# Weight sums on VectorE, mT evicted by two engines, a last turn of its own, and batch statistics in two parts: one change to a four-layer graph kernel

## The chip, the cores and the metric

The kernel runs on one core of a Trainium2 chip. The metric is device time in microseconds (us) of one execution. The kernel before the change takes 2664.24 us, the median of three runs from 2663.99 to 2666.74; the profiled execution spans 2665.5 us, and every time of a view below counts from its start.

## What is computed

x is 128 graphs of 128 nodes with 256 features, adj one 128 by 128 matrix, all in float32. Four layers follow each other, each as x = x + layer(relu(layernorm(x))). Cut to what matters:

```python
# layer 0: gated messages                       (h = relu(layernorm(x)))
m_in  = (a_in  @ h + eb ) * sigmoid(h @ gate_w)
m_out = (a_out @ h + oeb) * sigmoid(h @ out_gate_w)
x = x + relu(m_in + m_out + h * sigmoid(h @ loop_gate))
# layer 1: causal attention of one head, adj added to the scores
x = x + softmax(mask(q k^T / 16 + adj)) v Wo
# layer 2: three graph convolutions, 256 -> 512 -> 1024 -> 256
u = relu(A @ (h @ W1)); u = relu(A @ (u @ W2)); x = x + A @ (u @ W3)   # A = adj * adj
# layer 3: aggregate, linear, batchnorm, relu, linear, batchnorm
z = (A_hat @ h) @ bW1.T + b1;  z = relu(batchnorm(z))    # over all 128*128 rows
o = z @ bW2.T + b2;            x = x + batchnorm(o)
```

The two batch norms of layer 3 need mean and variance over all 16384 rows before their scale can be applied. So they cut the kernel into passes.

## The kernel before

**Tiling.** Four graphs make a group of T = 512 rows, and there are NG = 32 groups. Pass one takes every group through layers 0 to 2 and through the first linear of layer 3 (z); z goes to HBM except for the last group, 31, which stays in SBUF. Pass two takes z group by group (31 first, then 0 to 30: `ORDER`), applies the batch norm and relu on ScalarE, and multiplies by bW2; o stays in SBUF. Pass three applies the second batch norm, turns o by TensorE transposes, adds x3 and writes out.

**Seven products.** Every large product runs as seven half-size products on quarters (Winograd's form of Strassen's method) instead of eight. `seven` (L385) writes that list: seven matmul groups, with ScalarE copying three partial results (`kept`, L392) and VectorE or ScalarE putting four quarters together. The data side needs four elementwise sums (`sums`, L337, on VectorE). The weight side needs four more (`seven_of`, L198), made once per weight, on GpSimd: w1 (L263), w2 and w3 (L265, L266), the two attention weights (L259), bW1 (L294) and bW2 (L271).

**Streams and the written order.** Each layer is a generator that yields after each small step. One letter of a string takes one step of one generator: A and B are layers 0 and 1 (with the first part of layer 2) of later groups, C the rest of layer 2 of group g, D layer 3 of group g-1; b and d are the first step (the norm) of a further group of layers 1 and 3. `TURN` (L674) is the order for each of the 32 turns, `FILL` (L683) the order of the head, which brings the first groups to where turn 0 starts; there p is `prepare` (L237), which makes the weights ready. In turn 31 there is no A or B left, so that the same string leaves C, D and one d, and what remains of layer 3 of group 31 runs alone behind it (L701).

**The planner.** The order written is a priority, not a final order. At build time a planner puts each engine's instructions in a fixed sequence by estimated durations: what it believes ready may go ahead of earlier work that is not. In the trace the sum of L276, of the sixth step of `prepare`, runs at 9.95 us, ahead of work written long before it. On the chip each engine then works off its sequence in order.

**Names of the change.** `norm` (L305) takes mean and variance on VectorE (L311, L313), the inverse root on GpSimd (L315 to L319) and writes h by four ScalarE instructions (L322). `mixed` (L327) multiplies the node dimension by an adjacency matrix into a PSUM bank for each chunk of 128 features and evicts it; its callers give the engine: ScalarE for mT of layer 2's input (L561), VectorE for uT (L580) and gT (L648). `pu_x` to `pu_z` are the products of mT with W1. The first, pu_x, reads chunk 0 of mT, the second, pu_y, chunk 1, and the others their sums ms. `bn_affine` (L705) makes scale and shift from `bn_stats` rows, one of six numbers for each group, by one `bn_aggr` for each channel chunk (L710) over all 32 groups: four for the first batch norm (192 numbers each), two for the second.

The instructions of the mixed product with its eviction, and of a norm's end, are the ones that a reader should keep in view:

```python
pm[:, b, :], src[:, b, c * P : (c + 1) * P], aT        # L333, TensorE
evict(dst[:, c, :], pm.rearrange("p b n -> p (b n)"))    # L335
nc.scalar.activation(h[:, b, :], xt[:, b, :], AF.Relu, bias=..., scale=...)   # L322
```

Of the kernel before, what the change touches and what calls it, by code (L numbers as in the profile page):

```python
# [8 lines left out]
FP = mybir.dt.float32  # L9
AF = mybir.ActivationFunctionType  # L10
ALU = mybir.AluOpType
# [4 lines left out]
P = 128  # L16
LN_EPS = 1e-5
BN_EPS = 1e-5
# [4 lines left out]
def kernel(  # L23
# [39 lines left out]
    nc = tc.nc  # L63
    B, N, D = x.shape
    G = 4
    NG = B // G
    T = G * N
    DC = D // P
# [5 lines left out]
    FC = F1 // P  # L74
    assert N == P and T == 512 and D == 256 and H1 == 512 and B % G == 0

    const = ctx.enter_context(tc.tile_pool(name="const", bufs=1))
# [41 lines left out]
    a2T = const.tile([P, P], FP, name="a2T")  # L119
    ahT = const.tile([P, P], FP, name="ahT")  # L120
# [5 lines left out]
    stats1 = const.tile([P, FC, NG, 6], FP, name="stats1")  # L126
    stats2 = const.tile([P, DC, NG, 6], FP, name="stats2")
# [32 lines left out]
    an, anT, dscr, f = (part_of(wide1, P) for _ in range(4))  # L160
# [17 lines left out]
    for v in (b1, g1, be1, b2, g2, be2):  # L178
        k = v.shape[0] // P
# [3 lines left out]
    def inv_sqrt(dst, src, eps):  # L183

        if eps:
            nc.vector.tensor_scalar(dst, src, eps, None, ALU.add)
            src = dst
        nc.gpsimd.tensor_tensor(dst, src, nhalf[:, : dst.shape[1]], ALU.pow)
# [9 lines left out]
    def seven_of(b, name, extra=None):  # L198


        b11, b21, b12, b22 = quarters(b)
        if extra is None:
            extra = weights.tile([P, 3, b.shape[1] // 2, b.shape[2] // 2], FP, name=f"{name}_s")
        operands = set_of(b, extra)
        t4n, t1, t2 = operands[3:6]
        nc.gpsimd.tensor_tensor(t1, b12, b11, ALU.subtract)
        nc.gpsimd.tensor_tensor(t2, b22, t1, ALU.subtract)
        nc.gpsimd.tensor_tensor(t4n, b21, t2, ALU.subtract)
        nc.gpsimd.tensor_tensor(b12, b22, b12, ALU.subtract)
        return operands  # L210

    BW2T = scratch.tile([P, FC, D], FP, name="BW2T")
# [111 lines left out]
            )  # L324
        return h

    def mixed(dst, src, aT, name, evict):  # L327

        for c in range(src.shape[-1] // P):
            pm = bank([P, G, P], f"{name}_{c}")  # L330
            for b in range(G):
                nc.tensor.matmul(  # L332
                    pm[:, b, :], src[:, b, c * P : (c + 1) * P], aT, start=True, stop=True  # L333
                )
            evict(dst[:, c, :], pm.rearrange("p b n -> p (b n)"))  # L335

    def sums(engine, a, extra, s3=None):  # L337

# [137 lines left out]
    def layer1(g):  # L476
# [81 lines left out]
        h = norm(g, 2)  # L558
        yield
        mT = w.tile([P, DC, T], FP, tag="dT", name=f"mT_{g}", bufs=2)  # L560
        mixed(mT, h, a2T, f"pm2_{g}", nc.scalar.copy)  # L561
        ex = w.tile([P, 3, 1, T // 2], FP, tag="ex", name=f"ms_{g}", bufs=2)
        ms = sums(nc.vector, quarters_t(mT), ex)
        yield
# [12 lines left out]
            rows_by_half(ms, SETS["1"], H1 // 2), put, [P, 2, H1 // 2], f"pu_{g}"  # L577
        )
        uT = w.tile([P, HC1, T], FP, tag="uT", name=f"uT_{g}", bufs=1)
        mixed(uT, u, a2T, f"pmu_{g}", nc.vector.tensor_copy)  # L580
        ex = w.tile([P, 3, HC1 // 2, T // 2], FP, tag="us", name=f"us_{g}", bufs=1)
        US[g] = sums(nc.vector, quarters_t(uT), ex)
        yield
# [59 lines left out]
    def layer3(g):  # L643

        h = norm(g, 3)
        yield
        gT = w.tile([P, DC, T], FP, tag="dT", name=f"gT_{g}", bufs=2)
        mixed(gT, h, ahT, f"pg_{g}", nc.vector.tensor_copy)  # L648
        ex = w.tile([P, 3, 1, T // 2], FP, tag="ex", name=f"gs_{g}", bufs=2)
        gs = sums(nc.vector, quarters_t(gT), ex)  # L650
        yield
        z = ZT[g] = [zp.tile([P, 2, T], FP, tag="z", name=f"zo_{g}_{j}") for j in range(2)]
        done = []

        def put(ij, pb, other):
            i, j = ij
            dst = z[j][:, :, i * T // 2 : (i + 1) * T // 2]
            if other is None:
                nc.scalar.copy(dst, pb)
            else:  # L660
                nc.vector.tensor_tensor(dst, pb, other, ALU.add)
            done.append(j)
            if done.count(j) == 2:
                for jj in range(2):
                    nc.vector.bn_stats(stats1[:, 2 * j + jj, g, :], z[j][:, jj, :])
                if g != LAST:
                    nc.sync.dma_start(Z[g][:, 2 * j : 2 * j + 2, :], z[j])

        yield from seven(columns_by_half(gs, SETS["b"], 0), put, [P, 2, T // 2], f"pz_{g}")

    TURN = "CCCBCCABBDABBCABBDDCBADCDDBDCCDBACBCCABCCACbBCBBCBCBBCBCBCdB"  # L674
    US = {}
    AHEAD = 3

# [2 lines left out]

    FILL = "apaapaaaaBBABBBBBBBpBABBBApBABBpABBpABBABB"  # L683
    stream = {"a": layer0(0), "p": prepare(), "B": layer1(0), "A": part(layer0, 1)}
    for k in FILL:
        next(stream[k])
# [3 lines left out]
    for g in range(NG):  # L690
        if g + AHEAD < NG:
            load_x(g + AHEAD)
        stream = {
            "A": part(layer0, g + 2), "B": bs, "C": layer2(g), "D": ds,
            "b": part(layer1, g + 2), "d": layer3(g),
        }
        for k in TURN:
            next(stream[k], None)
        assert all(next(stream[k], k) == k for k in "ABCD")
        bs, ds = stream["b"], stream["d"]  # L700
    for _ in ds:  # L701
        pass
    passA.close()

    def bn_affine(stats, nch, gam, bet, name, bias=None):  # L705


        mv = const.tile([P, nch, 2], FP, name=f"mv_{name}")
        for j in range(nch):
            nc.vector.bn_aggr(mv[:, j, :], stats[:, j].rearrange("p g s -> p (g s)"))  # L710
        mean = mv[:, :, 0]
        if bias is not None:
            mean = const.tile([P, nch], FP, name=f"mean_{name}")
            nc.vector.tensor_tensor(mean, mv[:, :, 0], bias, ALU.add)
        sc = const.tile([P, nch], FP, name=f"sc_{name}")
        inv_sqrt(sc, mv[:, :, 1], BN_EPS)
        nc.vector.tensor_tensor(sc, sc, gam, ALU.mult)
        sh = const.tile([P, nch], FP, name=f"sh_{name}")
        nc.vector.tensor_tensor(sh, mean, sc, ALU.mult)
        nc.vector.tensor_tensor(sh, bet, sh, ALU.subtract)  # L720
        if bias is not None:
            part = const.tile([P, nch], FP, name=f"part_{name}")
            nc.vector.tensor_tensor(part, bias, sc, ALU.mult)
            nc.vector.tensor_tensor(sh, sh, part, ALU.add)
        return sc, sh


# [27 lines left out]
    def second(g):  # L755

        zl, zr = ZT[g]
        ex = zw.tile([P, 2, FC // 2, T // 2], FP, tag="zs", name=f"zs_{g}")
        a11, a21, a12, a22 = (z[:, :, i * T // 2 : (i + 1) * T // 2] for z in (zl, zr) for i in range(2))
        s1, s2 = ex[:, 0], ex[:, 1]  # L760
        a_r = a11, a12, a12, a22, s1, s2, a21
        for j in range(FC):
            z = ZT[g][j // 2][:, j % 2, :]
            nc.scalar.activation(  # L764
                z, z, AF.Relu, bias=sh1[:, j : j + 1], scale=sc1[:, j : j + 1],
            )
            yield
        nc.vector.tensor_tensor(s1, a21, a22, ALU.add)
        nc.vector.tensor_tensor(a21, a11, a21, ALU.subtract)
        nc.vector.tensor_tensor(s2, s1, a11, ALU.subtract)  # L770
        yield

        def product(r, pb, first):
            for c in range(FC // 2):
                nc.tensor.matmul(  # L775
                    pb, BW2R[r][:, c, :], a_r[r][:, c, :],
                    start=(first and c == 0), stop=(c == FC // 2 - 1), skip_group_check=True,
                )
            if r == 1:
                nc.vector.tensor_tensor(a12, a12, s2, ALU.subtract)  # L780

        done = []

        def put(ij, pb, other):
            i, j = ij
            dst = O[g][:, j, i * T // 2 : (i + 1) * T // 2]
            if other is None:
                nc.scalar.copy(dst, pb)
            else:
                nc.vector.tensor_tensor(dst, pb, other, ALU.add)  # L790
            done.append(j)
            if done.count(j) == 2:
                nc.vector.bn_stats(stats2[:, j, g, :], O[g][:, j, :])

        yield from seven(product, put, [P, T // 2], f"po_{g}", zw)

    for n in range(1, 1 + AT_ONCE):
        load_z(n)
    sc1, sh1 = bn_affine(stats1, FC, g1_c, be1_c, "bn1", b1_c)
    PREPARE = FC + 1  # L800
    now = second(LAST)
    for _ in range(PREPARE + 1):
        next(now)
    for n, g in enumerate(ORDER):
        then = second(ORDER[n + 1]) if n + 1 < NG else iter(())
        for _ in range(PREPARE):
            next(now)
            next(then, None)
        next(then, None)
        for _ in now:  # L810
            pass
        now = then
        if n + 1 + AT_ONCE < NG:
            load_z(n + 1 + AT_ONCE)
        if n % 4 == 3 and n // 4 < EARLY:
            load_x3(n // 4, x3p, "x3")
# [7 lines left out]

    for g in range(EARLY, EARLY + LATE):
        load_later(g)
    sc2, sh2 = bn_affine(stats2, DC, g2_c, be2_c, "bn2", b2_c)
    for g in range(NG):
        x3 = R[g]
        for i in range(DC):  # L830
# [52 lines left out]
```

## Time and profile before

| Part of the span | us | what runs |
|---|---|---|
| head, to the first product of turn 0 (first p_x of L377 at 98.57) | 98.6 | FILL |
| 32 turns | about 2252 | TURN; 71.65 us from turn to turn in the middle |
| end of pass one, from the last C step to the first po_x (2351 to 2380.5) | 29.5 | layer 3 of group 31, first batch norm |
| pass two (2380.5 to 2584.7) | 204 | 32 groups, some 6.2 us each |
| second batch norm and pass three (2584.7 to 2665.5) | 81 | transposes and writes; DMA at 322 GB/s or more from 2580 on |

The profile's first part gives TensorE (PE) 2541.2 us of 2665.5 (95%), VectorE (DVE) 1904.5 (71%), ScalarE (ACT) 1298.8 (49%), GpSimd (POOL) 317.0 (12%). A stretch in which PE is near its full length is read as bound by TensorE: there, other engines' work matters only if PE waits for it. In the view by stretches, PE is busy 71.04 of the 71.65 us of a middle turn, while it stands idle for some 50 of the first 140. The chain of waits names TensorE for 81% of the span. A line of the timeline reads: start, length, engine, line, operation, output<-inputs, shape, count, and in brackets the idle time before it with what ended it.

### The profile page before, as it was taken

Reading aid. Unit: us, or ns where it says so; the run is one execution under the profiler, and the core shown is the slowest. Engines: PE = TensorE matmul, PEld = TensorE weight load, DVE = VectorE, ACT = ScalarE, POOL = GpSimd, SP = SyncE. Lnnn points to the kernel's source line nnn. Section 1 sums busy time; section 2 is a strip of 40 time slices with the busy share of each in tenths; the row PEclk is TensorE's granted clock in tenths of the full one; section 3 lists DMA queues with packets and bytes.
Section 4 is the critical chain, followed back from the end, with each engine's and each line's share of the span. In section 5 each row is a group of like instructions: output and inputs, shape, how many; then the busy total and the mean of one; then the engine's idle time right before and its main releaser. Section 6 shows DMA issues by size and latency. Waiting matters only on the chain.

```text
span 2665.5 us, 40593 instructions
## 1 busy us (share of the span) xinstructions
PE 2541.2 (95%) x15215; PEld 2283.0 (86%) x15215; DVE 1904.5 (71%) x4743; ACT 1298.8 (49%) x2607; POOL 317.0 (12%) x616
## 2 busy tenths in 40 slices
PE   3899999999999999999999999999999999979984
PEld 2799999989998898999999899988989999968873
DVE  7677777777777777777777777777777776557775
ACT  3454444444455444454444444544454543336655
POOL 4111111111011110111111111111101111000011
PEclk7899999999999999999999999999999999989998
DMA  3000000000000000000000000000000000034469
GB/s 129 15 33 24 25 33 33 33 32 25 25 33 32 32 33 33 33 25 24 32 33 32 32 25 27 29 33 32 32 33 33 28 13 25 32 112 170 171 209 362
DMA packets 62055, 143.05 MB, mean 54 GB/s; under 512 B 4626, under 2 KB 39972, under 8 KB 57892
## 3 DMA queue, kind: packets, MB, share of 16 engines
q1 hardware_dynamic: 51636, 105.60, 11.1%
q0 software_dynamic: 9216, 33.56, 3.2%
q8 instruction: 120, 1.97, 0.3%
q10 hardware_dynamic: 1008, 1.31, 0.2%
q14 instruction: 75, 0.61, 0.1%
HBM read 73.48 MB, written 66.98 MB: 53 GB/s over the span
## 4 chain that ended last, share of the span: by engine, by line
PE 81%; DVE 6%; ACT 4%; DMA 4%; POOL 3%; issue 1%; ACTq 0%; POOLq 0%; DVEq 0%; SPq 0%
PE p_x L377 15%; PE p_z L377 8%; PE p_x L360 7%; PE pu_x L360 4%; PE pmu L332 4%; PE pz_x L377 4%; PE p_y L377 4%; PE po_x L775 3%; PE p_z L360 2%; ACT h L322 2%; PE pg L332 2%; PE pm L469 2%; PE py L551 2%; PE pqv_x L501 2%; PE pqv_x L496 2%; PE ps L521 2%
## 5 line engine op out<-in xcount | busy, mean ns | idle before, releaser
L322 ACT ACTIVATE h<-x,sh,rs 128x256 f32<-128x256 f32 x512 | 268.6, 589 | 386.4 <-POOL sh L319 386.4
L377 PE MATMUL p_x<-uT,w 128*128 128x256 f32 x1024 | 242.1, 379 | 0.0
L608 ACT ACTIVATE h2T<-h2T 128x512 f32<-128x512 f32 x192 | 120.4, 627 | 230.2 <-DVE h2T L607 230.2
L377 PEld LDWEIGHTS p_x<-uT,w 128*128 128x128 f32 x1024 | 189.6, 190 | 23.1
L315 POOL TENSOR_SCALAR rs<-mv 128x4 f32<-128x4 f32 x128 | 29.7, 232 | 1386.9 <-ACT h2T L608 1025.7
L311 DVE BATCH_NORM_STATS2 st<-x 128x6 f32<-128x256 f32 x512 | 190.4, 414 | 4.3 <-DMA x<-in_x_dram 2.1
L429 DVE SCALAR_TENSOR_TENSOR gs<-h,gw 128x256 f32<-128x256 f32 x384 | 163.3, 425 | 34.8 <-ACT h L322 28.8
L392 ACT COPY p_t<-p_x 128x512 f32<-128x512 f32 (+1 forms) x192 | 96.7, 504 | 114.6 <-PE p_x L377 101.9
L316 POOL TENSOR_TENSOR rs<-rs,nhalf 128x4 f32<-128x4 f32 x128 | 147.7, 1154 | 0.0
L332 PEld LDWEIGHTS pmu<-a2T,u 128*128 128x128 f32 x1024 | 119.5, 192 | 17.1 <-PE pr L636 7.4
L360 PEld LDWEIGHTS p_x<-w,h2T 128*128 128x128 f32 x1024 | 124.3, 192 | 3.3
L360 PE MATMUL p_x<-w,h2T 128*128 128x128 f32 x1024 | 124.6, 275 | 0.0
L574 ACT ACTIVATE u<-u 128x512 f32<-128x512 f32 x96 | 60.4, 631 | 131.8 <-DVE u L573 131.8
L764 ACT ACTIVATE zi<-zi,sh_bn,sc_bn 128x512 f32<-128x512 f32 x124 | 97.4, 812 | 55.4 <-DMA zi<-z 35.5
L332 PE MATMUL pmu<-a2T,u 128*128 128x128 f32 x1024 | 119.8, 275 | 1.8 <-ACT u L574 1.8
L377 PE MATMUL p_x<-us,w_s 128*128 128x256 f32 x512 | 121.3, 379 | 0.0
L377 PE MATMUL p_z<-us,w 128*128 128x256 f32 x512 | 121.2, 379 | 0.0
L377 PE MATMUL p_x<-uT,w_s 128*128 128x256 f32 x512 | 121.0, 379 | 0.0
L377 PE MATMUL p_y<-uT,w 128*128 128x256 f32 x512 | 121.0, 379 | 0.0
L377 PE MATMUL p_z<-us,w_s 128*128 128x256 f32 x512 | 121.0, 379 | 0.0
L377 PEld LDWEIGHTS p_z<-us,w 128*128 128x128 f32 x512 | 97.2, 190 | 13.5 <-ACT p_t L392 0.3
L377 PEld LDWEIGHTS p_z<-us,w_s 128*128 128x128 f32 x512 | 97.3, 190 | 13.2
(282 smaller groups left out, 6140.8 us busy)
## 6 DMA issues: line engine op xcount, KB each, us to landing
z<-zo SPq DMA_DIRECT2D x62, 512.0 KB, 2.6
zi<-z SPq DMA_DIRECT2D x31, 1024.0 KB, 4.8
x<-in_x_dram SPq DMA_DIRECT2D x32, 512.0 KB, 3.9
x<-x POOLq DMA_DIRECT2D x32, 512.0 KB, 3.0
x3i<-x POOLq DMA_DIRECT2D x32, 512.0 KB, 6.6
out_dram<-x3i SPq DMA_DIRECT2D x64, 256.0 KB, 8.3
w<-in_L_gnn_W_dram SPq DMA_DIRECT2D x1, 2048.0 KB
w<-in_L_gnn_W_dram SPq DMA_DIRECT2D x1, 1024.0 KB
```

Source lines behind the costliest of these rows:

```text
L311: nc.vector.bn_stats(st[:, b, :], xt[:, b, :])
L316: nc.gpsimd.tensor_tensor(rs, rs, nhalf[:, :G], ALU.pow)
L322: nc.scalar.activation(h[:, b, :], xt[:, b, :], AF.Relu, bias=sh[:, b : b + 1], scale=rs[:, b : b + 1])
L332: nc.tensor.matmul(pm[:, b, :], src[:, b, c * P : (c + 1) * P], aT, start=True, stop=True)
L360: nc.tensor.matmul(pb[:, rr, :], a_r[r][:, c, rr * P : (rr + 1) * P], b_r[r][:, c, :wide], start=(first and rr == 0 and c == 0), stop=(c = ...
L377: nc.tensor.matmul(pb[:, jj, :], b_r[r][:, c, at : at + P], a_r[r][:, c, :], start=(first and jj == 0 and c == 0), stop=(c == nk - 1), ski ...
L392: nc.scalar.copy(t, pb)
L429: nc.vector.scalar_tensor_tensor(gs, h[:, b, :], 1.0, gw[:, i, :], ALU.mult, ALU.mult, accum_out=gl[:, b, i : i + 1],)
L574: nc.scalar.activation(dst, dst, AF.Relu)
L608: nc.scalar.activation(dst, dst, AF.Relu)
L764: nc.scalar.activation(z, z, AF.Relu, bias=sh1[:, j : j + 1], scale=sc1[:, j : j + 1],)
L775: nc.tensor.matmul(pb, BW2R[r][:, c, :], a_r[r][:, c, :], start=(first and c == 0), stop=(c == FC // 2 - 1), skip_group_check=True,)
```

## The change

It has four edits. `seven_of` makes its four sums on VectorE instead of GpSimd, and `FILL` is a new order for the head. mT is evicted in turns by VectorE (chunk 0) and ScalarE (chunk 1) instead of ScalarE alone, so that the chunks need not queue on one engine. Turn 31 gets its own string, `FINAL`: it keeps layer 3 of group 30 (D) back, to run it among the steps of layer 3 of group 31 (d), which ran alone before. And the batch statistics of 31 groups are aggregated ahead (`most1`, `most2`), so that after the last group only its own six numbers are aggregated (`last1`, `last2`) and merged by a formula of a few small operations.

```diff
 def seven_of(...)
-        nc.gpsimd.tensor_tensor(t1, b12, b11, ALU.subtract)
-        nc.gpsimd.tensor_tensor(t2, b22, t1, ALU.subtract)
-        nc.gpsimd.tensor_tensor(t4n, b21, t2, ALU.subtract)
-        nc.gpsimd.tensor_tensor(b12, b22, b12, ALU.subtract)
+        nc.vector.tensor_tensor(t1, b12, b11, ALU.subtract)
+        nc.vector.tensor_tensor(t2, b22, t1, ALU.subtract)
+        nc.vector.tensor_tensor(t4n, b21, t2, ALU.subtract)
+        nc.vector.tensor_tensor(b12, b22, b12, ALU.subtract)
...
 def mixed(...)
-            evict(dst[:, c, :], pm.rearrange("p b n -> p (b n)"))
+            evicts[c % len(evicts)](dst[:, c, :], pm.rearrange("p b n -> p (b n)"))
...
-        mixed(mT, h, a2T, f"pm2_{g}", nc.scalar.copy)
+        mixed(mT, h, a2T, f"pm2_{g}", (nc.vector.tensor_copy, nc.scalar.copy))
...
+    def bn_part(stats, nch, groups, name):
+        mv = const.tile([P, nch, 2], FP, name=f"mv_{name}")
+        for j in range(nch):
+            nc.vector.bn_aggr(mv[:, j, :], stats[:, j, groups].rearrange("p g s -> p (g s)"))
+        return mv[:, :, 0], mv[:, :, 1]
...
     TURN = "CCCBCCABBDABBCABBDDCBADCDDBDCCDBACBCCABCCACbBCBBCBCBBCBCBCdB"
+    FINAL = "CCCCCCCCCCCCCCCCCCDCCDCCDdDDdDddDdDdddd"
...
-    FILL = "apaapaaaaBBABBBBBBBpBABBBApBABBpABBpABBABB"
+    FILL = "paaapaaaAaBBBBBABBBBBBBppABBAApBBABBBpBBAB"
...
-        for k in TURN:
+        for k in TURN if g < LAST else FINAL:
             next(stream[k], None)
...
+    most1 = bn_part(stats1, FC, slice(LAST), "most1")
     for _ in ds:
         pass
...
-    def bn_affine(stats, nch, gam, bet, name, bias=None):
-        for j in range(nch):
-            nc.vector.bn_aggr(mv[:, j, :], stats[:, j].rearrange("p g s -> p (g s)"))
+    def bn_affine(most, last, nch, gam, bet, name, bias):
+        (mean, var), (mean1, var1) = most, last
+        share = 1.0 / NG
+        nc.vector.tensor_tensor(d, mean1, mean, ALU.subtract)
+        nc.vector.scalar_tensor_tensor(mean, d, share, mean, ALU.mult, ALU.add)
+        nc.vector.tensor_tensor(mean, mean, bias, ALU.add)
+        nc.vector.scalar_tensor_tensor(d, d, share * (1.0 - share), d, ALU.mult, ALU.mult)
+        nc.vector.scalar_tensor_tensor(d, var, 1.0 - share, d, ALU.mult, ALU.add)
+        nc.vector.scalar_tensor_tensor(var, var1, share, d, ALU.mult, ALU.add)
...
-                nc.vector.bn_stats(stats2[:, j, g, :], O[g][:, j, :])
+                nc.vector.bn_stats(stats2[:, j, (g + 1) % NG, :], O[g][:, j, :])
...
+    last1 = bn_part(stats1, FC, slice(LAST, NG), "last1")
+    sc1, sh1 = bn_affine(most1, last1, FC, g1_c, be1_c, "bn1", b1_c)
...
+        if n + 1 == NG:
+            most2 = bn_part(stats2, DC, slice(LAST), "most2")
...
+    last2 = bn_part(stats2, DC, slice(LAST, NG), "last2")
+    sc2, sh2 = bn_affine(most2, last2, DC, g2_c, be2_c, "bn2", b2_c)
```

The slot of `stats2` moves by one because pass two begins with group 31, so that its last group, 30, must lie in the last slot.

## The prediction

> **What bounds the kernel now.** I read the page's slices first, for the shape of the span.
>
> ```profile
> PE   3899999999999999999999999999999999979984
> DVE  7677777777777777777777777777777776557775
> PEclk7899999999999999999999999999999999989998
> ```
>
> Each digit is a fortieth of the span, 66.6 us. TensorE is full from the third digit to the 7, and VectorE is not: anything that doesn't end a wait of TensorE there is worth nothing. TensorE is slack in three places: the head (digits 3 and 8, at a reduced clock), the end of pass one (the 7), and the last stage, which the DMA row fills. Next I asked the waits for TensorE alone, from 160 to 2340 us. One answer came:
>
> ```profile
> PE pu_x L360 <- ACT mT L335: 17.9, 29, 0.6
> ```
>
> So the turns hold one single stall, 29 times 0.62 us. The timeline shows what it costs: a stalled turn, then turn 30, which has no stall.
>
> ```profile
> 2218.44 1.95 PE L360 MATMUL p_z<-w_s,h2s 128*128 128x128 f32 x16
> 2221.01 1.13 PE L360 MATMUL pu_x<-w,mT 128*128 128x256 f32 x4 [0.62 <-ACT mT L335]
> 2221.97 1.03 PE L360 MATMUL pu_y<-w,mT 128*128 128x256 f32 x4
> ...
> 2287.93 1.95 PE L360 MATMUL p_z<-w_s,h2s 128*128 128x128 f32 x16
> 2289.72 1.03 PE L360 MATMUL pu_x<-w,mT 128*128 128x256 f32 x4
> 2290.58 1.03 PE L360 MATMUL pu_y<-w,mT 128*128 128x256 f32 x4
> ```
>
> From the start of p_z to that of pu_y it takes 3.53 us against 2.65: a stall costs 0.88 us, not 0.62, since an end as shown includes the drain of the pipeline and pu_x's first weights load late. Who holds mT back is seen in any turn of the middle:
>
> ```profile
> 1071.84 0.42 DVE L624 TENSOR_TENSOR s<-p_y,p_t 128x256 f32<-128x256 f32 x1
> 1072.02 2.07 ACT L322 ACTIVATE h<-x,sh,rs 128x256 f32<-128x256 f32 x4 [2.75 <-POOL sh L319]
> 1073.99 1.04 ACT L335 COPY mT<-pm 128x512 f32<-128x512 f32 x2
> 1075.07 0.42 DVE L343 TENSOR_TENSOR ms<-mT 128x256 f32<-128x256 f32 x1 [2.81 <-ACT mT L335]
> ```
>
> pm (start 1070.26) is done by 1072.05, but ScalarE first writes a norm's h (step b, written just ahead) until 1074.09. VectorE stands idle for those 2.81 us.
>
> The head, timeline of VectorE and GpSimd:
>
> ```profile
> 23.05 0.41 DVE L449 SCALAR_TENSOR_TENSOR m<-aout,gt,m 128x128 f32<-128x128 f32 x1
> ...
> 24.45 2.43 DVE L449 SCALAR_TENSOR_TENSOR m<-aout,gt,m 128x128 f32<-128x128 f32 x1
> ```
>
> ```profile
> 24.21 2.52 POOL L206 TENSOR_TENSOR w_s<-w 128x1024 f32<-128x1024 f32 x1
> ```
>
> The same instruction takes 0.41 or 2.43 us; the long one ends when GpSimd's sum of w2 ends. The chain of waits runs through exactly these rows (L449, L452, L457) from 22.5 to 39.3 us.
>
> The end of pass one:
>
> ```profile
> 2359.21 2.07 ACT L322 ACTIVATE h<-x,sh,rs 128x256 f32<-128x256 f32 x4 [4.94 <-POOL sh L319]
> 2359.86 3.78 PE L332 MATMUL pg<-ahT,h 128*128 128x128 f32 x16 [4.41 <-ACT h L322]
> ...
> 2372.55 1.89 DVE L710 BATCH_NORM_AGGREGATE mv_bn<-stats 128x2 f32<-128x192 f32 x2
> ```
>
> TensorE waits 4.41 us for the norm of group 31, then runs at half speed (pg takes 3.78 us, 1.95 in the turns).
>
> **What the Trainium skill says.** "SBUF — State Buffer", section "Who interferes with whom": a VectorE instruction with two SBUF inputs contends with a GpSimd instruction that reads SBUF, and the second to issue blocks wholly until the first ends. The trace agrees: 2.43 us instead of 0.41. "TensorE: Matmul & The Clock Gate", section "What's actually happening": an idle TensorE falls to half its clock. It agrees: PEclk is 0.50 from 30 to 50 us, pg doubles. For prices, "VectorE: DVE Perf Modes", section "The TRN2 errata", gives a float32 two-input operation (N+151)/0.96 ns: 1.22 us at 1024, 0.29 at 128; the trace has 1.22 (L473) and 0.29 (L233).
>
> **Part by part.**
>
> mT by two engines: VectorE gets 0.69 us a turn (row L335, gT), ScalarE loses 0.58. Chunk 0 is in PSUM by about 1071.2; VectorE is free at 1072.26 behind L624 and done by 1072.95. pu_x, which reads chunk 0, then starts right behind p_z at 1072.04+1.79=1073.83, 0.78 earlier. Behind the copy stand VectorE's sums ms, which wait for chunk 1 anyway. pu_y reads chunk 1, still behind h on ScalarE: ready at 1073.99+0.58=1074.57, needed at 1074.69, with its weight load some 0.2 before, at 1074.5. So up to 0.14 of the 0.88 may stay. I take 0.80: 29 x 0.80 = **23 us**; ends 0.62 x 29 = 18 and 0.88 x 29 = 25.5. TensorE keeps its written order p_z, pu_x, pu_y (C, B, B in TURN).
>
> The head. Contention gone, the stretch 22.5 to 39.3 (16.8 us) becomes 4 x (0.35+0.35+0.48)=4.7 by the rows of group 1 (63 to 68 us), or about 5, since ScalarE feeds it: saves 11.8. The twelve L429 before it took 8.4 us (12.96 to 21.35) against 12 x 0.47=5.6: saves 2.5 (some is other work). VectorE takes on the sums: q and v 8 x 0.29=2.3, w1 4 x 0.42=1.7, w2 4 x 1.22=4.9, w3 4 x 0.69=2.8, the two of layer 3 8 x 0.42=3.4, together 15.1 us. Only q's and v's are written into this stretch, half of them beside waits: costs 1.2; the planner may put a long sum of w2 just before a due instruction: another 1.2. So layer 0 of group 0 ends some 12 us earlier. Then, from 45.9 to 98.6 us, layer 1 is a chain of latencies, with VectorE busy for about 33 of 53: the 12.8 us of w1 to bW2 fit in its gaps. The new FILL writes most of group 1's layer 0 behind these steps: the softmax exponent no longer waits for group 1's gates (66.67 against 65.2 possible: 1.4), and the u sums no longer for L463 and L471 (92.5 against some 88: 3). Against it, GpSimd's norm chain now meets VectorE's two-input sums: in the turns L316 takes 1.56 for 1.04 and L318 0.78 for 0.23, so 1 us for each of two norms, and 1 for blocked puts. 12+4.4-3 = 13.4; to this the warmer clock adds 1 to 2. I take **15 us**; ends 4 (all 15.1 on the path, less 2 of shadow, against 11.8+2.5+4.4) and 22.
>
> The last turn: six of layer 3's seven products of group 30 (0.865 each, from the spacing of pz rows) move from before the last pr to behind it: pr ends 5.2 earlier. They fill the 4.41 us wait, so the clock stays up: pg saves 1.8, the first pz 1.1. On VectorE the puts and bn_stats of group 30 now stand among those of 31 with the four big bn_aggr (0.94 each): from the first of these on, about 13.6 us of work where 11.5 lie, so some 2 us come back. Group 31's z uses the two buffers of group 30's, whose write to HBM takes 2.6 us (page, part 6); behind its first put stand the other puts, but three products need none, so I cost it 0 to 2. Sum 5.2+2.9-2-1=5.1, plus the pz stalls of 0.4+0.3+0.8 partly filled: **6 us**; ends 2 and 9.
>
> Statistics ahead: after the last put, bn_stats waited from 2373.1 to 2374.35 behind an aggregate and then two more took 1.89. Those 3.1 us go; 4 small aggregates (0.36, as L313) and five dependent small operations at 0.2 come: saves **1.7**. For the second norm 1.02 goes and as much comes, and GpSimd's issues hold the root until 2587.9 anyway: 0. most2's 2 us lie in the last group's gaps on VectorE (78% busy). Pass three is DMA work and only shifts.
>
> Sum 23+15+6+1.7 = 45.7: 2664.2-45.7 = **2618.5 us**.
>
> **Rivals.** (A) VectorE becomes the bound of the head: it is busy 98 of the first 140 us, and 15 are added; but about 17 of the 98 were blocked time. Head 4: 2629.5. (B) The stall passes to pu_y: chunk 1 has 0.1 us to spare. If 0.6 remains, 0.28 x 29=8: 2633.5. (C) Both: 2644.5. (D) Slower: the planner, with mT ready earlier in its estimate, moves pu_x and pu_y ahead of p_z. Then pu_x waits 0.9 for the copy and pu_y 0.8 for chunk 1, 1.7 instead of 0.88 a turn, +24, with a head of 4 and no gain in the tail: 2684. Against it speaks that the order of the turns is as written. (E) Everything at its good end: 2606.
>
> **How the numbers follow.** Forecast 0.57, A 0.14, B 0.13, C 0.05, D 0.05, E 0.04, and 0.02 for a mix of C and D that cancels. The range goes from E to past B, 2606 to 2637, and leaves out C, D and the mix. Faster: forecast, A, B, C and E, 0.93; same: the mix, 0.02; slower: D, 0.05.
>
> **What would show it.** Right: no TensorE wait on mT in the turns, and a turn-to-turn distance of 70.8 to 71.0 instead of 71.65; L449 at 0.35 throughout and the first p_x of L377 at about 83 instead of 98.57; the wait for group 31's h under 1 us; L710's successors before the last group at 0.94, after it under 0.1. Wrong: a wait of pu_y on ScalarE of over 0.3 (B), VectorE full from 12 to 80 us with TensorE waiting for it (A), or pu_x ahead of p_z (D).

## The result, and the profile after

The changed kernel takes 2621.74 us, the median of four runs from 2620.70 to 2622.09, against 2665.49 (2663.99 to 2667.18) for the kernel before beside it. The ratio is 0.9835, with a 95% interval from 0.9818 to 0.9852. The profiled spans are 2620.1 and 2665.5 us. The forecast was 2618.5, its range 2606 to 2637.

To see where the 45.4 us came from, I cut both spans at three marks of the chain of waits: the first `pmu` of turn 0, the first `pmu` of turn 30 (the last turn that brings a group through layer 1), and the first `po_x` of pass two.

| stretch | before | after | gained | forecast |
|---|---|---|---|---|
| start to pmu of turn 0 | 158.32 | 144.11 | 14.2 | 15 |
| 29 turns, to pmu of turn 29 (71.65 and 70.79 each) | 2077.86 | 2052.88 | 25.0 | 23 |
| turn 29 to turn 30 | 68.61 | 68.68 | -0.1 | 0 |
| pmu of turn 30 to po_x | 75.72 | 69.51 | 6.2 | 6 + 1.7 |
| po_x to the end | 284.99 | 284.92 | 0.1 | 0 |

One caution: the last row, a pass two that is full of TensorE's work (203 of 205 us in the changed kernel) and a pass three that is full of transfers, took 282.8 to 285.0 us over all fourteen profiles of this study. The first row, too, differs from profile to profile: in eight profiles with one and the same head it ended at 143.77 to 146.30 us, and VectorE's first step, which waits for the first x, started at 7.15 to 8.35 us over all fourteen. So a difference of under 2 us between two medians says little. Below I read the marks. Of two marks of the head, too, a difference of under 2.5 us says little, while the turns of one profile agree within 0.01 us.

**The page's slices** of the changed kernel, each digit a fortieth of the span (65.5 us):

```profile
PE   4999999999999999999999999999999999989984
DVE  7777777777777777777777777777777776567775
PEclk8999999999999999999999999999999999999997
```

The first two digits of PE are 4 and 9 instead of 3 and 8, the 7 of the 36th digit, the end of pass one, is an 8, and the clock (the third row) has no 8 there any more. The page has TensorE at 97% instead of 95%, and the chain of waits names it for 92% of the span instead of 81%.

**A turn**, timeline of the changed kernel:

```profile
1047.29 0.42 DVE L624 TENSOR_TENSOR s<-p_y,p_t 128x256 f32<-128x256 f32 x1
...
1047.46 2.08 ACT L322 ACTIVATE h<-x,sh,rs 128x256 f32<-128x256 f32 x4 [2.75 <-POOL sh L319]
1047.49 1.95 PE L360 MATMUL p_z<-w_s,h2s 128*128 128x128 f32 x16
1047.63 0.68 DVE L335 COPY mT<-pm 128x512 f32<-128x512 f32 x1
...
1049.28 1.03 PE L360 MATMUL pu_x<-w,mT 128*128 128x256 f32 x4
1049.45 0.56 ACT L335 COPY mT<-pm 128x512 f32<-128x512 f32 x1
...
1050.14 1.05 PE L360 MATMUL pu_y<-w,mT 128*128 128x256 f32 x4
```

VectorE copies chunk 0 while ScalarE still writes h, and pu_x stands directly behind p_z. From p_z to pu_y it is 2.65 us, as in the turn of before that had no stall. Asked for TensorE's waits from 160 to 2300 us, the trace names none for the matmuls. For the weight loads, which the engine list has as PEld, it names some short ones that no other engine ended (`issue`), one of 0.3 us, and this:

```profile
PEld pu_y L360 <- ACT mT L335: 4.4, 29, 0.2
```

Chunk 1 is ready at 1050.01, and pu_y's weights load 0.15 to 0.2 us late for it. The matmul behind them starts on time all the same, within 0.02 us (e8 below).

**The head**, VectorE in the changed kernel, in order of time:

```profile
22.36 0.34 DVE L449 SCALAR_TENSOR_TENSOR m<-aout,gt,m 128x128 f32<-128x128 f32 x1
...
24.22 0.61 DVE L449 SCALAR_TENSOR_TENSOR m<-aout,gt,m 128x128 f32<-128x128 f32 x2
...
26.01 0.69 DVE L463 COPY m<-pc 128x512 f32<-128x512 f32 x1
...
34.57 1.82 DVE L206 TENSOR_TENSOR w_s<-w 128x1024 f32<-128x1024 f32 x2
36.31 1.22 DVE L207 TENSOR_TENSOR w_s<-w,w_s 128x1024 f32<-128x1024 f32 x1
```

No L449 is blocked (0.34; two of them 0.61). L463 starts at 26.01 us, where it started at 39.32 before. The sums of w2 (L206, L207) come later, while TensorE waits for layer 1's norm anyway.

**The end of pass one**, timeline of the changed kernel:

```profile
2315.29 2.07 ACT L322 ACTIVATE h<-x,sh,rs 128x256 f32<-128x256 f32 x4 [1.60 <-POOL sh L319]
2315.94 1.20 PE L332 MATMUL pg<-ahT,h 128*128 128x128 f32 x8 [1.45 <-ACT h L322]
...
2323.74 0.98 DVE L675 BATCH_NORM_AGGREGATE mv_most<-stats 128x2 f32<-128x186 f32 x1
...
2325.91 1.13 PE L377 MATMUL pz_x<-gT,bw1T_s 128*128 128x256 f32 x4 [1.10 <-DVE zo L661]
...
2329.85 0.97 DVE L675 BATCH_NORM_AGGREGATE mv_most<-stats 128x2 f32<-128x186 f32 x1
2330.74 0.31 DVE L675 BATCH_NORM_AGGREGATE mv_last<-stats 128x2 f32<-128x6 f32 x4
...
2335.18 2.07 PE L787 MATMUL po_x<-zo,bw2T 128*128 128x256 f32 x4 [8.14 <-ACT zo L776]
```

The wait for group 31's h is 1.45 instead of 4.41 us, and eight matmuls of pg take 1.20 where sixteen took 3.78: the clock is up (granted 1.00 from 2315 to 2320 us, against 0.50 from 2360 to 2365 before). But the aggregates "ahead" are not ahead. The last of the four big ones starts at 2329.85, behind the puts of group 31, and one has pushed a put so far back that TensorE waits 1.10 us for it, where it waits 0.79 in the kernel before and in e5, which have no aggregates there. That is the step of the prediction that failed.

### The profile page after: what moved, and what is told of

Its sections match the earlier page's. It is cut to its first block, busy times and chain, and to the rows that moved or that the text cites. A ratio compares the mean times of both kernels' runs of the same rounds, so it can differ in the third digit from the quotient of the medians.

```text
span 2620.1 us, 40636 instructions
## 1 busy us (share of the span) xinstructions
PE 2531.6 (97%) x15215; PEld 2276.4 (87%) x15215; DVE 1917.9 (73%) x4819; ACT 1284.0 (49%) x2575; POOL 291.9 (11%) x588
## 4 chain that ended last, share of the span: by engine, by line
PE 92%; DMA 4%; ACT 2%; DVE 1%; issue 1%; POOL 0%; ACTq 0%; DVEq 0%; POOLq 0%; SPq 0%
PE p_x L377 17%; PE p_x L360 9%; PE p_z L377 8%; PE pmu L332 4%; PE p_z L360 4%; PE pu_x L360 4%; PE p_y L377 4%; PE pz_x L377 4%; PE po_x L787 3%; PE pm L332 2%; PE pg L332 2%; PE ps L521 2%; PE py L551 2%; PE pqv_x L501 2%; PE p_y L360 2%; PE pm L469 2%
## 5 line engine op out<-in xcount | busy, mean ns | idle before, releaser
L377 PE MATMUL p_x<-uT,w 128*128 128x256 f32 x1024 | 242.2, 379 | 0.0
L377 PEld LDWEIGHTS p_x<-uT,w 128*128 128x128 f32 x1024 | 189.7, 190 | 23.1
L429 DVE SCALAR_TENSOR_TENSOR gs<-h,gw 128x256 f32<-128x256 f32 x384 | 161.0, 419 | 28.4 <-ACT h L322 23.0
L316 POOL TENSOR_TENSOR rs<-rs,nhalf 128x4 f32<-128x4 f32 x128 | 148.9, 1163 | 0.0
L332 PEld LDWEIGHTS pmu<-a2T,u 128*128 128x128 f32 x1024 | 119.5, 192 | 15.1 <-issue 14.8
L377 PE MATMUL p_x<-us,w_s 128*128 128x256 f32 x512 | 121.2, 379 | 0.0
L377 PE MATMUL p_x<-uT,w_s 128*128 128x256 f32 x512 | 121.1, 379 | 0.0
L377 PE MATMUL p_y<-uT,w 128*128 128x256 f32 x512 | 121.1, 379 | 0.0
L377 PE MATMUL p_z<-us,w_s 128*128 128x256 f32 x512 | 121.0, 379 | 0.0
L377 PE MATMUL p_z<-us,w 128*128 128x256 f32 x512 | 121.0, 379 | 0.0
L637 DVE TENSOR_TENSOR x<-pr,x 128x512 f32<-128x512 f32 x64 | 43.7, 683 | 90.4 <-PE pr L636 90.4
L377 PEld LDWEIGHTS p_z<-us,w 128*128 128x128 f32 x512 | 97.3, 190 | 13.2
```

Of the source, the lines that this page charges most:

```text
L316: nc.gpsimd.tensor_tensor(rs, rs, nhalf[:, :G], ALU.pow)
L332: nc.tensor.matmul(pm[:, b, :], src[:, b, c * P : (c + 1) * P], aT, start=True, stop=True)
L377: nc.tensor.matmul(pb[:, jj, :], b_r[r][:, c, at : at + P], a_r[r][:, c, :], start=(first and jj == 0 and c == 0), stop=(c == nk - 1), ski ...
L429: nc.vector.scalar_tensor_tensor(gs, h[:, b, :], 1.0, gw[:, i, :], ALU.mult, ALU.mult, accum_out=gl[:, b, i : i + 1],)
```

## The experiments

Times are medians of four runs (five for e6) beside runs of the kernel before; ratios are to that kernel, with the 95% interval. "The mark" is the first pmu of turn 0, "the last stretch" that from the first pmu of turn 30 to the first po_x. Line numbers in a fence are those of the kernel named.

| kernel | us | ratio | mark | turn | last stretch |
|---|---|---|---|---|---|
| before | 2665.49 | 1 | 158.32 | 71.65 | 75.72 |
| changed | 2621.74 | 0.9835 (0.9818 to 0.9852) | 144.11 | 70.79 | 69.51 |
| e1, mT by ScalarE | 2646.88 | 0.9932 (0.9917 to 0.9947) | 144.40 | 71.66 | 69.51 |
| e7, engines of the chunks swapped | 2647.07 | 0.9932 (0.9915 to 0.9948) | 146.30 | 71.65 | 69.51 |
| e8, mT by VectorE | 2620.64 | 0.9834 (0.9820 to 0.9849) | 143.77 | 70.77 | 69.73 |
| e2, sums on GpSimd | 2635.59 | 0.9891 (0.9876 to 0.9906) | 159.21 | 70.79 | 69.78 |
| e3, old order of the head | 2626.22 | 0.9855 (0.9842 to 0.9869) | 150.54 | 70.79 | 69.51 |
| e10, only w2's and w3's sums on VectorE | 2629.23 | 0.9865 (0.9851 to 0.9880) | 152.49 | 70.79 | 69.77 |
| e11, e10 with dinv first | 2630.36 | 0.9866 (0.9851 to 0.9881) | 152.66 | 70.81 | 69.84 |
| e12, e2 with dinv first | 2634.62 | 0.9884 (0.9867 to 0.9900) | 158.03 | 70.79 | 69.78 |
| e4, no FINAL | 2624.27 | 0.9847 (0.9834 to 0.9861) | 145.38 | 70.79 | 72.99 |
| e5, statistics in one part | 2620.18 | 0.9832 (0.9819 to 0.9846) | 144.32 | 70.79 | 69.36 |
| e6, 30 groups ahead | 2621.92 | 0.9837 (0.9823 to 0.9850) | 145.32 | 70.78 | 69.28 |
| e9, 30 ahead in the last turn, z behind bw2T | 2619.64 | 0.9829 (0.9813 to 0.9846) | 145.97 | 70.79 | 67.36 |

### The eviction of mT: e1, e7, e8

```diff
-        mixed(mT, h, a2T, f"pm2_{g}", (nc.vector.tensor_copy, nc.scalar.copy))
+        mixed(mT, h, a2T, f"pm2_{g}", (nc.scalar.copy,))                          # e1
+        mixed(mT, h, a2T, f"pm2_{g}", (nc.scalar.copy, nc.vector.tensor_copy))    # e7
+        mixed(mT, h, a2T, f"pm2_{g}", (nc.vector.tensor_copy,))                   # e8
```

e1 undoes this edit alone.

> The changed kernel, but mT evicted by ScalarE alone, as before. Theory (the turns were held by one wait of TensorE on mT, and only the eviction's place removes it): the distance from turn to turn goes back from 70.79 to 71.65 us, the wait of pu_x on mT shows 29 times with 0.62 us, and the kernel takes 25 us more, some 2647 us. Rival (the turns got shorter because the other edits shifted the planner's order): 2622 to 2627 us, turns at 70.8.

e7 still spreads the two chunks over two engines, but gives the first to ScalarE.

> The changed kernel with the two engines of mT swapped: chunk 0 on ScalarE, chunk 1 on VectorE. The load of each engine is that of the changed kernel. Theory (what counts is that chunk 0, which the first product reads, isn't behind the norm's h on ScalarE): pu_x waits for ScalarE as before, turns of 71.5 to 71.65 us, 2643 to 2647 us. Rival (what counts is that ScalarE has 0.58 us less a turn, or that two engines share the work): turns of 70.8 us, 2622 us.

e8 takes ScalarE out altogether.

> The changed kernel with both chunks of mT on VectorE. Theory (chunk 1 on ScalarE is just in time, and VectorE has room): turns of 70.76 to 70.79 us, time within 1.5 us of the changed kernel's, about 2621 us. Rival (VectorE, 73% busy, can't take another 0.69 us a turn without holding something up): turns above 70.9, over 2625 us.

e1 and e7 agree: 71.66 and 71.65 us a turn, and times within 0.2 us of each other. In both, the waits of TensorE from 160 to 2300 us have the one line that the kernel before had. This is e7's:

```profile
PE pu_x L360 <- ACT mT L335: 17.9, 29, 0.6
```

So it is not the sharing that gains, nor ScalarE's 0.58 us, but that chunk 0, which pu_x reads, leaves the engine that is writing h. With e8 the late weight load of pu_y goes too, and the turn is 70.77 instead of 70.79: chunk 1 on ScalarE costs 0.02 a turn, 0.6 in the whole, and the medians do not tell the two apart.

### The head: e2, e3, e10, e11, e12

e2 puts all weight sums back on GpSimd; e3 keeps them on VectorE, but takes the old FILL.

```diff
-        nc.vector.tensor_tensor(t1, b12, b11, ALU.subtract)      # and the three others
+        nc.gpsimd.tensor_tensor(t1, b12, b11, ALU.subtract)      # e2
...
-    FILL = "paaapaaaAaBBBBBABBBBBBBppABBAApBBABBBpBBAB"
+    FILL = "apaapaaaaBBABBBBBBBpBABBBApBABBpABBpABBABB"          # e3
```

> The changed kernel with the weight sums back on GpSimd; the new order of the head stays. Theory (the two engines block each other in the head, and the new order is worth only some 3 us): VectorE's L449 and L452 take 2.4 us again where a sum of w2 runs, the head ends 9 to 13 us later, 2631 to 2635 us. Rival (the order of the head made the gain): 2 to 5 us later, 2624 to 2627 us.

> The changed kernel with the head's old order; the weight sums stay on VectorE. Theory (the two parts of the head are nearly additive: blocking some 11 us, order some 3): the head ends 2 to 5 us later than in the changed kernel, 2624 to 2627 us. Rival (VectorE can take the sums only in the new order; in the old one they stand on the path): 8 to 15 us later, 2630 to 2637 us.

The parts do not add. In the new order of the head the sums' engine is worth 15.1 us (159.21 to 144.11), more than the 9 to 13 expected; in the old order 7.8 (158.32 to 150.54). The order is worth 6.4 with the sums on VectorE and -0.9, which is nothing by the caution above, with them on GpSimd. Part of this is plain in e3's timeline of VectorE, behind the eviction L463 that feeds TensorE's pm:

```profile
27.53 1.21 DVE L207 TENSOR_TENSOR w_s<-w,w_s 128x1024 f32<-128x1024 f32 x1
29.78 0.69 DVE L471 TENSOR_TENSOR m<-pm,m 128x512 f32<-128x512 f32 x1 [1.03 <-PE pm L469]
30.38 1.22 DVE L208 TENSOR_TENSOR w_s<-w,w_s 128x1024 f32<-128x1024 f32 x1
31.52 0.68 DVE L471 TENSOR_TENSOR m<-pm,m 128x512 f32<-128x512 f32 x1
32.12 1.22 DVE L209 TENSOR_TENSOR w<-w 128x1024 f32<-128x1024 f32 x1
33.25 1.22 DVE L473 SCALAR_TENSOR_TENSOR x<-m,x 128x1024 f32<-128x1024 f32 x1
```

In the old order the planner has w2's sums between the last steps of layer 0 of group 0: L473 starts at 33.25 us, in the changed kernel at 31.18, where w2's sums come behind it. That is 2.1 us; the loss grows to 6.4 by the mark. There more sums and group 1's steps stand among those of layer 1, but which of them cost the rest was not followed up.

Why the order is worth nothing beside GpSimd's sums is another matter. My first thought was that only the long sums harm. e10 leaves just those of w2 and w3 on VectorE.

```diff
-    def seven_of(b, name, extra=None):
+    def seven_of(b, name, extra=None, eng=nc.gpsimd):
...
-        SETS["2"] = seven_of(w2, "w2")
-        SETS["3"] = seven_of(w3, "w3")
+        SETS["2"] = seven_of(w2, "w2", eng=nc.vector)
+        SETS["3"] = seven_of(w3, "w3", eng=nc.vector)
```

> The changed kernel with the weight sums of w2 and w3 on VectorE as in it, and those of the other five weights (q, v, w1, W2 and W1 of the block) on GpSimd as before. Theory (what costs in the head is that GpSimd's sums of the first two weights run beside VectorE's first norms and sums of x and stretch both; the later ones lie beside a TensorE that has its operands): the first pmu of turn 0 starts at 144 to 147 us, and the time is 2621 to 2624. Rival (every GpSimd sum that runs beside a norm or a put costs about its own length): the first pmu is over 150, and the time 2627 or more.

Theory wrong: the mark is 152.49, 8.4 late, and the number is the rival's. But no L449 is stretched here. In e10's timeline of VectorE the delay shows as a wait:

```profile
22.64 0.47 DVE L286 TENSOR_SCALAR wide<-wide,dinv 128x128 f32<-128x128 f32 x1 [4.66 <-POOL dinv L188]
```

The power `dinv` stands on GpSimd behind w1's and q's sums and a norm. In the new order VectorE's gate sums of group 0 (L429) are queued behind L286. In the kernel before, dinv stood ahead of those sums and the wait was 0.4. e11 and e12 write the degrees and dinv ahead of the sums of q and v:

```diff
+        nc.vector.tensor_tensor(an, adj_sb, ident, ALU.add)      # and the rest of the degrees
+        inv_sqrt(dinv, deg[:, 3:4], 0.0)
         SETS["q"], SETS["v"] = seven_of(m_qk, "m_qk"), seven_of(w_vo, "w_vo")
```

> As e10 (sums of w2 and w3 on VectorE, the other five weights' on GpSimd), with the degrees and the power dinv emitted ahead of the sums of q and v, so that the power comes before GpSimd's sums of w1 in GpSimd's order. Theory (what e10 lost is a queue: VectorE sat 4.7 us at L286 for dinv, which stood behind eleven sums and a norm on GpSimd): that wait falls under 0.5, the first pmu of turn 0 starts at 146.5 to 149.5 us instead of 152.5, time 2623.5 to 2626.5. Rival (contention for the buffers, by whatever GpSimd runs beside VectorE): the wait falls too, but the first pmu stays at 151 to 154 and the time at 2628 to 2631, since the same sums run beside the same work.

> As e2 (all weight sums on GpSimd in the new order of the head), with the power dinv ahead of GpSimd's sums in the same way. Theory (the new order's poor worth beside GpSimd's sums, -0.9 us against 6.4 beside VectorE's, is the 4.0 us that VectorE waited for dinv): the first pmu starts at 154.5 to 156.5 us instead of 159.2, time 2631 to 2633.5. Rival (x of the first group waits for VectorE's work that GpSimd's long sums of w2 hold up, dinv or not): the first pmu stays at 158 to 160, time 2634.5 to 2636.5.

The wait at L286 is gone in both, and nearly nothing is gained: 152.66 for 152.49, 158.03 for 159.21. The numbers are those of the rivals, but in e11 the mechanism is not the contention that its rival named. e11's timeline of ScalarE shows what took the wait's place:

```profile
22.51 1.10 ACT L322 ACTIVATE h<-x,sh,rs 128x256 f32<-128x256 f32 x2 [5.25 <-POOL sh L319]
```

ScalarE has the second group's norm ahead of the gates of group 0, and GpSimd works off q's sums between the steps of that norm (L316 ends at 20.8, its last step L319 runs only at 22.28). So the gates, and with them L457, come at 26.96 us instead of 21.96. It is the same queue, with another engine standing in it.

In e12, L457 does come earlier, at 26.73 us for 32.04 in e2, and GpSimd's long sums take it back, as e12's rival had it: L463 starts at 41.60 for 42.16. In all three kernels with these sums on GpSimd its last sum of w3 ends between 39.1 and 40.0 us, and L463 comes at 39.32 (before), 41.60 (e12) or 42.16 (e2), whether the first L457 stood at 22.50, 26.73 or 32.04. So up to L463 the order can gain little there.

e12 against e11 then measures the contention by itself: one order up to L463, and only w2's and w3's sums on another engine. Here is e12's VectorE, and then its GpSimd:

```profile
27.57 2.43 DVE L449 SCALAR_TENSOR_TENSOR m<-aout,gt,m 128x128 f32<-128x128 f32 x1
29.92 2.56 DVE L429 SCALAR_TENSOR_TENSOR gs<-h,gw 128x256 f32<-128x256 f32 x1
...
32.41 2.41 DVE L452 SCALAR_TENSOR_TENSOR m<-ident,gt,m 128x128 f32<-128x128 f32 x1
```

```profile
27.44 2.41 POOL L207 TENSOR_TENSOR w_s<-w,w_s 128x1024 f32<-128x1024 f32 x1
29.81 2.38 POOL L209 TENSOR_TENSOR w<-w 128x1024 f32<-128x1024 f32 x1
32.16 2.52 POOL L208 TENSOR_TENSOR w_s<-w,w_s 128x1024 f32<-128x1024 f32 x1
```

Each VectorE instruction ends with one GpSimd sum, whatever its own length. From the first L457 to L463 it takes 14.9 us in e12 (26.73 to 41.60) and 4.0 in e11 (26.96 to 30.99), so contention costs **10.8 us**. The 13.9 us between the marks of e12 and the changed kernel (158.03-144.11) then fall into three stretches: 10.8 of contention; 4.8 up to L457, which starts at 21.96 instead of 26.73, with no sum in GpSimd's queue; less 1.7 behind L463 (116.4 us to the mark in e12, 118.1 in the changed kernel). The first is firm: from L457 to L463 it takes 4.0 us in all eight profiles with the changed kernel's head. There L457 starts at 20.89 to 21.96, which makes the second 4.8 to 5.8. The last is not: it takes 118.1 to 121.0 there, and that VectorE's sums are what costs time behind L463 is not shown. Nor can the second be had without the first, as the 39.32 of the kernel before shows.

### The end of pass one: e4, e5, e6, e9

```diff
-        for k in TURN if g < LAST else FINAL:
+        for k in TURN:                                            # e4
...
-    most1 = bn_part(stats1, FC, slice(LAST), "most1")
-    last1 = bn_part(stats1, FC, slice(LAST, NG), "last1")
+    all1 = bn_part(stats1, FC, slice(0, NG), "all1")              # e5, no merge; the second norm alike
...
+        if g == LAST:                                             # e6, share 2/32 in the merge
+            most1 = bn_part(stats1, FC, slice(LAST - 1), "most1")
+    last1 = bn_part(stats1, FC, slice(LAST - 1, NG), "last1")
```

> The changed kernel without the last turn's own order; the statistics stay in two parts. Theory (the end of pass one gained 6.2 us through the last turn; but without it group 30's statistics are known long before the end, so that the split then gains what it should, 2 to 3 us): from the last uT product of pass one to the first product of pass two 72 to 74 us against 69.5 in the changed kernel and 75.7 before; 2624 to 2626 us. Rival (the split gains nothing anywhere): 75 to 76 us, 2627 to 2628 us.

> The changed kernel with the statistics of all 32 groups aggregated at the end, as before; the last turn's own order stays. Theory (with that order group 30's numbers come so late that the four big aggregates run on VectorE among the last puts, and the split brings nothing): the same stretch stays at 69.0 to 70.0 us, time within 0.6 us of the changed kernel's. Rival (the split shortens the path by the 1.7 us of the prediction or more): 71.2 us or more, 1.7 to 3 us slower.

> The changed kernel with the first statistics cut elsewhere: 30 groups are aggregated ahead, from the start of the last turn on, and the last two at the end (weights 30/32 and 2/32). Theory (VectorE is what the end of pass one waits for, and the four big aggregates are 3.9 us of its work there): the same stretch falls from 69.5 to 66.5 to 67.6 us, 2619 to 2620 us. Rival (TensorE's own chain or GpSimd's root sets the end): 69 to 70 us, no change.

Without FINAL the last stretch is 72.99, so the split alone gains 2.7 (75.72 to 72.99); without the split it is 69.36, so FINAL alone gains 6.4. Together they gain 6.2. With FINAL, the split gains nothing (-0.15): group 30's statistics are only there when group 31's puts run, so the aggregates of 31 groups can start no earlier.

e6 takes group 30 out of them. The aggregates went, but the planner put them into turn 30, which grew by 0.7 (69.39 instead of 68.68), and the last stretch gained only 0.2. What ends it now is a transfer, in e6's timeline:

```profile
2328.67 0.34 ACTq L750 DMA_DIRECT2D bw2T<-BW2T  x1
...
2336.86 2.04 PE L787 MATMUL po_x<-zo,bw2T 128*128 128x256 f32 x4 [8.23 <-DMA bw2T<-BW2T]
```

The load of bW2's turned form takes 8.2 us for 512 KB. Three z loads of 1 MB each are issued some 4 us before it. e5 shows the same wait, and so do e2, e8, e10, e11 and e12: their end of pass one is the changed kernel's, and for this load alone their last stretch is 69.73 to 69.84 instead of 69.51. e9 mends both: the aggregates are tied to group 31's h2T, the output of its second convolution, so that they can't go into turn 30, and the second and third z load wait for bw2T.

```diff
+            if g == LAST and i == 8:      # mv is first written by ScalarE from h2T of group 31
+                most1 = bn_part(stats1, FC, slice(LAST - 1), "most1", H2[LAST][:, 0, :FC])
...
+        if n in (2, 3):
+            nc.scalar.copy(z[:, 0, 0:1], bw2T[:, 0, 0:1])
```

> The changed kernel with 30 groups aggregated ahead (two of 32 left), the aggregates tied to the last group's h so that they can be done only inside the last turn, and the loads of the z chunks 2 and 3 made to start after the load of the second weight of W2's second half. Theory (after the last weight gradients the first po waits for VectorE's aggregates in the changed kernel and for that load in the kernels that moved them): neither wait is left, the stretch from the last turn's first pmu to the first po_x goes from 69.5 us to 67 to 68.3, turn 30 is back at 68.7, and the time is 2618.5 to 2620.5. Rival (the load only shares the bandwidth with what else is on the way, and lands when it did): the stretch stays at 69.2 to 69.6 and the time at 2620.5 to 2622.5. Second rival (the delayed z chunks are what pass two then waits for): the stretch is shorter, but the time 2622 or above.

(Its "last weight gradients" are group 31's products of z, and the weight that it speaks of is bw2T.)

As the theory has it: turn 30 is back at 68.68, the last stretch is 67.36, and the time 2619.64. e9's timeline shows bw2T read by the small copy 3.3 us after its issue, and po_x held by ScalarE's zo alone:

```profile
2328.63 0.34 ACTq L753 DMA_DIRECT2D bw2T<-BW2T  x1
...
2331.97 0.28 ACT L764 COPY zi<-bw2T 128x1 f32<-128x1 f32 x2 [2.76 <-DMA bw2T<-BW2T]
...
2334.89 2.07 PE L792 MATMUL po_x<-zo,bw2T 128*128 128x256 f32 x4 [6.31 <-ACT zo L781]
```

By this mark e9 beats the changed kernel by 2.15 us. Its median is 2.1 lower, but its head began 1.9 later in the profiled run, and the intervals of the two ratios overlap: the marks show the gain, the times do not yet.

## Why the prediction was right, and where it was not

**The turns** (23 forecast, 25.0 measured): right in its mechanism, and a term of the sum was mis-sized. It was 0.80 of a stall's 0.88, with up to 0.14 left to pu_y. The 0.88 itself is borne out by the 0.86 that went: an idle time of 0.62 in the trace is not the whole of a stall, since p_z is shown 1.95 us long though the next product can start 1.79 behind its start, and pu_x's row is 0.10 longer with its weights late. The shortfall of chunk 1 is there, 0.15 to 0.2 us in the weight load, but the load runs ahead of its matmul by about as much, so it cost 0.02 (e8). That is the good end of the forecast. Rivals B, C and D are out: no wait of pu_y over 0.3, no pu_x ahead of p_z.

**The head** (15 forecast, 14.2 measured, 12.0 to 14.6 with the marks of the eight profiles): right in the sum and for the greater part right in the steps. From the first L457 to L463 it takes 4.05 us instead of 16.8, a gain of 12.8 where 11.8 was forecast; "Who interferes with whom" (the Trainium skill, "SBUF — State Buffer") said that the one which issues second blocks until the other ends, and e12's three pairs show just that. The 2.5 for the twelve L429 was as good as lost: L457 starts only 0.5 earlier (21.96 for 22.50) though the first L429 starts 0.7 earlier (12.23 for 12.96), since the eight sums of q and v now stand between those instructions, and I had charged 1.2 for them. The order's 4.4 against 3 and the clock's 1 to 2 were to give some 3 us behind layer 0; from L473 on, 0.8 came (13.4 gained there, 14.2 at the mark). The prediction also took engine and order for separate sums, and they are not: with the sums left on GpSimd the new order gains nothing, because L463 comes only when GpSimd's sums are done. The low end of 4 is not the sum of the terms that it names, which give 18.7-13.1 = 5.6. Rival A is out: VectorE is busy for 53 of the 70 us from 10 to 80. First p_x of L377: 84.55, forecast about 83.

**The last turn** (6 forecast; FINAL alone 6.4): right. pr ends 5.9 us earlier, counted from turn 30's pmu (forecast 5.2). Group 31's h gains only 4.8 of it, since its norm now comes in one piece behind pr and a put of group 30: the wait is 1.45, where I said under 1. The clock's gain is there, as "What's actually happening" (the Trainium skill, "TensorE: Matmul & The Clock Gate") has it for a TensorE that isn't idle: granted 1.00 instead of 0.50 in the 5 us from group 31's pg on. From h to po_x 1.6 us go in e5 (21.30 to 19.73), most likely by the clock; no run parts it from the other order of the products.

**The split of the statistics** (1.7 forecast, -0.15 measured): this step failed. I costed it on the profile of before, where group 30 is long done when group 31 ends, and for that profile the credit was even too low: e4 has 2.7. But the same change moves group 30's products behind the last pr, and I had written there that four aggregates of 0.94 would stand among the last puts; I booked their 2 us against FINAL and still credited the split in full. "L710's successors before the last group at 0.94" was the sign to look for, and it is absent. From group 31's h to zo, which no load holds up, it takes 18.58 us in e5, 19.03 in the changed kernel and 16.88 in e9, where the aggregates run ahead as they were meant to. So the split was worth the 1.7 of the forecast, and at the place where it came to stand it cost 0.45. At po_x only 0.15 of that is seen, since in e5 bw2T comes 0.3 late. The size was right, the place was not. For the second norm, 0 was forecast, and the last two passes differ by 0.1.

The profiled spans differ by 45.4 us and the medians by 43.8, where 45.7 was forecast. The sum is that good because terms cancel: the turns gave 2.0 more and FINAL 0.4, the split 1.9 less and the head 0.8.

## What to carry to other kernels

Ask of a shared eviction which chunk the next product reads first, and give that one to the engine that is free: here that decided, not the balance. When an edit moves work off a slow engine, look for what was queued behind that work as well as for what it blocked: here contention was 10.8 us and the queue some 5, and giving dinv its place in the queue by itself gained nothing. And cost two edits of one stretch on the schedule that both leave behind, not each on the old one.

## What was not expected of the hardware

A VectorE instruction of 12 elements a partition is held as long as a large one. In e2's timeline of VectorE:

```profile
27.11 2.18 DVE L435 TENSOR_TENSOR gl<-gl,gb 128x12 f32<-128x12 f32 x1
```

It takes 0.17 us in the changed kernel. The blocking also goes the other way, for which the prediction had charged 1 us a norm: in the changed kernel GpSimd's small steps of a norm meet VectorE's sums, in its timeline of GpSimd:

```profile
34.82 1.06 POOL L318 TENSOR_SCALAR sh<-mv 128x4 f32<-128x4 f32 x1
35.85 1.45 POOL L316 TENSOR_TENSOR rs<-rs,nhalf 128x4 f32<-128x4 f32 x1
```

They take 0.23 and 1.04 in the kernel before at 2357.7 us, beside an idle VectorE, so this norm came 1.2 us late; in e10 one L316 took 1.98. And a load of 512 KB took 8.2 us behind three of 1 MB that were issued 4 us earlier, and 3.3 with two of these held back.
